# The last pair's gate and rest turned to token rows by VectorE, GpSimd and DMA instead of TensorE

## The chip, the cores and the metric

The kernel runs on one core of a Trainium2 chip. The metric is device time in microseconds (us): the median of the runs of one program. A profile is one more execution, taken by the hardware profiler; its span runs from the first to the last instruction, and the device time of the same execution is a little longer. The engines are TensorE (PE in the profile; its weight loads are PEld), VectorE (DVE), ScalarE (ACT), GpSimd (POOL) and SyncE (SP, which only issues DMAs here). ACT and POOL issue DMAs too. A `q` behind an engine's name in the profile (SPq, ACTq) means its instruction queue.

## The reference

Eight sequences of 512 tokens with 256 features, all float32. Cut to what matters:

```python
nx = layer_norm(x, gamma, beta)
evidence = softmax((nx @ Wq) @ (prototypes @ Wk).T / 16) @ (prototypes @ Wv)
combined = concat([nx, evidence, anchor])             # 768 features
probs = softmax(combined @ router_W + router_b)       # 3 experts
h = silu(combined @ e_w1[e] + e_b1[e])                # 512 hidden features an expert
routed = sum_e probs[e] * (h[e] @ e_w2[e] + e_b2[e])
g = sigmoid(silu(combined @ gate_w1 + gate_b1) @ gate_w2 + gate_b2)
out = x + g * (routed @ out_w + out_b)
```

## The kernel before

The work goes over four pairs of sequences, j = 0 to 3. Within a pair the activations lie with features on the 128 partitions and the 512 tokens along the free dimension, and the big matrix products are made as a 2x2 block scheme over the two sequences of the pair (rows 0 and 1) and the two halves of the features, with seven block products in place of eight; sums and differences of blocks are made by VectorE. `e_w2` and `out_w` are multiplied into one weight beforehand, so that after the hidden layer one more layer of products, in `outputs`, gives `routed @ out_w`.

`outputs(j, steps)` begins with the gate (`hg` tiles, a sigmoid on ACT), and then makes the four results of the pair: `r11` (first half of the features, sequence 0), `r12` (first half, sequence 1), `r21` (second half, sequence 0), `r22` (second half, sequence 1). Each starts as a bias sum on ACT, and TensorE adds block products in PSUM banks `u`, `z`, `y`, twelve products of 128x512 each (`experts`, which calls `product`, L945, twice for each of six steps over the three experts). Two results share bank `u` one after the other: the product for `r22` is added in, VectorE reads it, and then the product for `r21` is added on top of it in the same bank. VectorE adds a bank to its result, multiplies with the gate, turns the result by 32x32 blocks (a stream transpose), and GpSimd adds `x`, which lies in a tile `xb` in the same blocked form (`finish`, L1430 to 1437). `store` (L1425) writes it to the output with four DMAs of 64 KB, in pieces of 128 bytes.

In the first three pairs all four results go this way. The last pair (j = 3) has an order of its own, which the change touches. There `r11`, the first 128 features of sequence 6, is finished with tokens on the partitions, so that it needs no turning at the end: `token_experts` multiplies one 128-token tile of the hidden layer with the weights, twelve products of 128x128 into one PSUM bank, four tiles in all. `finish_rows` then multiplies the bank with the gate (L1511), adds the rest (L1512), both on VectorE, and stores a tile of 128 tokens by one DMA of 64 KB (L1513), tiles 0 and 2 from ACT's queue, tiles 1 and 3 from SP's. "Rest" is what does not wait for this product: `x + gate * (bias sum and the other products of r11)`. The gate and the rest have features on the partitions, and have to be turned to token rows first. Before the change `finish_early` (L1439 to 1445) makes the rest on VectorE (a block transpose of `xb`, a multiplication, an addition), and `turn_rest` (L1494) turns gate and rest on TensorE: eight transposes of 128x128 into two PSUM banks, which ACT copies to the tile `rest` (L1502). `turn_rest` stands between the product for `r22` and the last sum, that for `r21`; the token products follow the last sum. `r21` has been prepared by `finish_early` as well, and `finish_late` (L1452) multiplies the last sum with the gate in place (tile `hg`), adds, turns by blocks, and stores by two DMAs from ACT's queue and two from SP's. The token rows lie in a tile `y_rows` that takes over one of the two buffers `yb`, from which `r12` has been stored.

The order of the work: each engine carries out its instructions in the order in which the code issues them (`manual_schedule`), and the framework puts in the waits between engines, on semaphores. A DMA is issued by an engine's queue when its waits are over, and what stands behind it in that queue waits with it. The DMAs that SP and ACT issue count on eight semaphores, which the framework deals round in the order in which its own plan places the DMAs; a DMA that gets a semaphore whose last owner may not be done yet waits for that owner to land.

Of the kernel before, what the change touches and what calls it, by code (L numbers as in the profile page):

```python
# [8 lines left out]
F32 = mybir.dt.float32  # L9
AF = mybir.ActivationFunctionType  # L10
ALU = mybir.AluOpType
# [5 lines left out]
def kernel(  # L17
# [51 lines left out]
    nc = tc.nc  # L69
    P = 128  # L70
    B, T, H = x.shape
# [3 lines left out]
    NT = T // P  # L75
# [11 lines left out]
    dram = ctx.enter_context(tc.tile_pool(name="dram", bufs=2, space=bass.MemoryType.DRAM))  # L87
# [3 lines left out]
    work = ctx.enter_context(tc.tile_pool(name="work", bufs=2))  # L91
# [8 lines left out]
    def bank(i, name):  # L100
        ps = psum.tile([P, 512], F32, tag=f"b{i}", name=name)
        bank_of[ps.name] = i
        return ps
# [4 lines left out]
    def misc(name):  # L108
        spare.append(spare.pop(0))
        return bank(spare[-1], name)  # L110
# [6 lines left out]
    ident = const.tile([P, P], F32, tag="ident", name="ident")  # L117
# [15 lines left out]
    TB = 32  # L133
# [68 lines left out]
    r = 0  # L202
# [373 lines left out]
    S = {}  # L576
# [366 lines left out]
    def product(ps, lhsT, rhs, start=False):  # L943

        return nc.tensor.matmul(ps, lhsT, rhs, start=start, stop=True, skip_group_check=not start)  # L945
# [46 lines left out]
    def hidden(j, q, k, i):  # L992
        return S["h", i, 2 * q // RC][:, (2 * q + k) % RC, :]
# [344 lines left out]
    def outputs(j, steps):  # L1338
# [7 lines left out]
        hg = [[S["hg", i, k] for i in range(2)] for k in range(2)]  # L1346
# [14 lines left out]
        u, z, y = (bank(i, f"ps_g{n}_{j}") for n, i in (("u", 0), ("z", 2), ("y", 4)))  # L1361
# [23 lines left out]
        def a(q, i, k):  # L1385
            return w2o[:, 2 * q + k, i * P : (i + 1) * P]

        def experts(ps, lhs, k, i, start=False):
            for q in range(NQ):
                product(ps, lhs(q), hidden(j, q, k, i), start=start and q == 0)  # L1390

        def combo(s):
            return lambda q: w2s[:, s, q, :]
# [11 lines left out]
        def bias_sum(role, i, row):  # L1405

            r = work.tile([P, T], F32, tag=role, name=f"{role}_{j}", bufs=1)
            nc.scalar.activation(
                by_side(r), pb[:, row, :, 1, :], AF.Identity, bias=b2o[:, i, 0:1],
                scale=b2o[:, i, 1:2],  # L1410
            )
            for e in range(2, E):
                nc.vector.scalar_tensor_tensor(
                    by_side(r), pb[:, row, :, e, :], b2o[:, i, e : e + 1], by_side(r), ALU.mult, ALU.add
                )
            return r
# [13 lines left out]
        def finish(r, ps, i, row):  # L1430

            yb = work.tile([P, T], F32, tag="yb", name=f"yb_{2 * j + row}_{i}")
            nc.vector.tensor_tensor(r, r, ps, ALU.add)
            nc.vector.tensor_tensor(r, r, S["hg", row, i], ALU.mult)
            nc.vector.transpose(yb, r)  # L1435
            nc.gpsimd.tensor_tensor(yb, yb, S["xb", 2 * j + row][:, i, :], ALU.add)  # L1436
            store(yb, i, row, slice(0, T), (nc.sync,))

        def finish_early(r, i, row):  # L1439

            xb = S["xb", 2 * j + row][:, i, :]
            yb = work.tile([P, T], F32, tag="yb", name=f"yb_{2 * j + row}_{i}")
            nc.vector.transpose(yb, xb)
            nc.vector.tensor_tensor(r, r, S["hg", row, i], ALU.mult)
            nc.vector.tensor_tensor(r, r, yb, ALU.add)
# [6 lines left out]
        def finish_late(r, ps, i, row):  # L1452
# [5 lines left out]
        r11, r22, r12, r21 = (  # L1458
            bias_sum(f"r{i + 1}{row + 1}", i, row) for i, row in ((0, 0), (1, 1), (0, 1), (1, 0))
        )  # L1460
        ug = u
        u, y, z = (bank(i, f"ps_{n}2_{j}") for i, n in ((1, "u"), (3, "y"), (5, "z")))
# [15 lines left out]
        if j + 1 < NP:  # L1478
# [12 lines left out]
            run("P4")  # L1491
            return

        def turn_rest(r):  # L1494

            rest = work.tile([P, 2, NT, P], F32, tag="xg", name="rest", bufs=1)
            for n, part in enumerate((S["hg", 0, 0], r)):
                pt = misc(f"pt_rest_{n}")
                for t in range(NT):
                    ts = slice(t * P, (t + 1) * P)  # L1500
                    nc.tensor.transpose(pt[:, ts], part[:, ts], ident)
                nc.scalar.copy(rest[:, n, :, :].rearrange("p t c -> p (t c)"), pt)  # L1502
            return rest

        def token_experts(ps, t):

            for q in range(NQ):
                product(ps, hidden(j, q, 1, 0)[:, t * P : (t + 1) * P], a(q, 0, 1), start=q == 0)

        def finish_rows(y, rest, ps, t, queue):  # L1510
            nc.vector.tensor_tensor(y, ps, rest[:, 0, t, :], ALU.mult)  # L1511
            nc.vector.tensor_tensor(y, y, rest[:, 1, t, :], ALU.add)  # L1512
            queue.dma_start(out[2 * j, t * P : (t + 1) * P, :P], y)  # L1513

        subtract((0, 1), ((1, 0), (0, 1)))
        experts(z, combo(S4), 1, 1)
        finish_early(r11, 0, 0)
        finish_early(r21, 1, 0)
        finish(r12, z, 0, 1)
        experts(u, lambda q: a(q, 1, 0), 0, 0)  # L1520
        finish(r22, u, 1, 1)
        rest = turn_rest(r11)
        experts(u, lambda q: a(q, 1, 1), 0, 1)
        tokens = [bank(b, f"ps_tokens_{b}")[:, :P] for b in (2, 0, 5, 3)]
        for t in range(NT):
            token_experts(tokens[t], t)
        finish_late(r21, u, 1, 0)
        y = work.tile([P, NT, P], F32, tag="yb", name="y_rows")
        for t in range(NT):
            finish_rows(y[:, t, :], rest, tokens[t], t, nc.sync if t % 2 else nc.scalar)  # L1530


    with tc.manual_schedule(engines=None):
# [85 lines left out]
        for j in range(NP):  # L1619
# [79 lines left out]
            gate_layer(j, within)  # L1699
            half_layers(j)  # L1700
            outputs(j, between)


# [32 lines left out]
```

## Time and profile before

| what | time |
|---|---|
| median of 3 runs | 455.69 us (455.13 to 455.75) |
| the profiled execution, device time | 454.99 us |
| the profiled execution, span | 453.2 us |
| TensorE busy | 448.6 us, 99% of the span |
| VectorE busy | 363.8 us, 80% |
| ACT busy | 214.5 us, 47% |
| GpSimd busy | 96.8 us, 21% |
| mean granted TensorE clock | 1.0 |

The rows of the profile below have the start in us from the beginning of the span, the length in us, the engine, the line of the kernel, the operation, the tiles it writes and reads (out<-in), shapes as partitions x elements, and how many instructions were merged. In brackets stands how long the engine was idle before, and what ended that. The chain of waits is followed back from the last instruction: at each step to what released it, or to the instruction before it on its engine. The waits of SP's queue have the total, the count and the longest.

### The profile page before, as it was taken

To read this page: it belongs to the slowest core of one execution; us is meant where nothing else is said; L and a number is where in the kernel's file an instruction comes from. 1 tells how busy PE (TensorE), PEld (TensorE's weight loads), DVE (VectorE), ACT (ScalarE), POOL (GpSimd) and SP (SyncE) were. 2 spreads that over 40 slices of the span, in tenths; PEclk is the share of its full clock that TensorE was granted. 3 is DMA by queue.
4 is the path that set the end of the run, shared out by engine and by line. 5 is a ranking of instruction groups with operands and counts; after the bars stand their busy time and mean duration, and the time that the engine had idled before them with its cause. 6 is when DMAs were issued, how large, how long until landed. Compare 5 with 4: busy or idle time off the path is not lost.

```text
span 453.2 us, 5537 instructions
## 1 busy us (share of the span) xinstructions
PE 448.6 (99%) x1801; PEld 214.4 (47%) x1801; DVE 363.8 (80%) x698; ACT 214.5 (47%) x378; POOL 96.8 (21%) x157
## 2 busy tenths in 40 slices
PE   9999999999999999999999999999999999999996
PEld 7554444754444444444444544444444444444445
DVE  2878999949698899769789899777979956677983
ACT  3545875463501675466230476658330355557000
POOL 6466600342432200001331310000151310000010
PEclk9999999999999999999999999999999999999999
DMA  8984682354012477203002248301102291000014
GB/s 254 385 177 114 104 251 40 59 124 45 1 29 41 118 176 146 51 0 47 7 10 36 47 154 166 54 0 29 25 0 47 48 210 23 1 0 0 1 17 76
DMA packets 119956, 35.32 MB, mean 78 GB/s; under 512 B 106076, under 2 KB 116376, under 8 KB 119928
## 3 DMA queue, kind: packets, MB, share of 16 engines
q1 hardware_dynamic: 115344, 27.02, 29.0%
q0 software_dynamic: 2656, 7.16, 4.9%
q10 hardware_dynamic: 1928, 0.80, 0.7%
q8 instruction: 14, 0.23, 0.2%
q14 instruction: 14, 0.11, 0.1%
HBM read 27.56 MB, written 7.39 MB: 77 GB/s over the span
## 4 chain that ended last, share of the span: by engine, by line
PE 99%; DVE 0%; issue 0%
PE ps_u L945 45%; PE ps_z L945 20%; PE ps_y L945 14%; PE ps_gu L945 3%; PE ps_vw L824 3%; PE ps_w2o L547 2%; PE ps_s L691 2%; PE ps_gz L945 2%; PE ps_tokens L945 1%; PE ps_late_u L945 1%; PE ps_wake L316 1%; PE ps_v L356 1%; PE ps_m L356 1%; PE ps_gy L945 1%; PE ps_late_z L945 1%; PE pt_x L619 0%
## 5 line engine op out<-in xcount | busy, mean ns | idle before, releaser
L945 PE MATMUL ps_u<-nxT,w 64*128 64x512 f32 (+1 forms) x208 | 96.6, 591 | 0.0
L1024 DVE TENSOR_TENSOR h<-h,pb 128x512 f32<-128x512 f32 x96 | 62.8, 687 | 13.7 <-ACT h L981 13.6
L945 PE MATMUL ps_u<-h,w2o 128*128 128x512 f32 x144 | 63.9, 593 | 0.0
L981 ACT ACTIVATE h<-h,abias 128x512 f32<-128x512 f32 x72 | 49.1, 717 | 27.6 <-DVE h L987 27.6
L945 PE MATMUL ps_y<-nxT,w 64*128 64x512 f32 (+1 forms) x104 | 51.4, 589 | 0.0
L945 PE MATMUL ps_z<-T,ws 64*128 64x512 f32 (+1 forms) x104 | 51.4, 590 | 0.0
L945 PE MATMUL ps_z<-nxT,ws 64*128 64x512 f32 (+1 forms) x104 | 51.3, 589 | 0.0
L945 PEld LDWEIGHTS ps_u<-nxT,w 64*128 64x128 f32 (+1 forms) x208 | 37.2, 187 | 26.4 <-issue 23.1
L945 PE MATMUL ps_u<-T,ws 64*128 64x512 f32 (+1 forms) x104 | 49.4, 589 | 0.0
L945 PE MATMUL ps_u<-T,w 64*128 64x512 f32 x112 | 48.4, 590 | 0.0
L945 PEld LDWEIGHTS ps_u<-h,w2o 128*128 128x128 f32 x144 | 27.3, 190 | 32.8 <-issue 32.3
L945 PE MATMUL ps_z<-h,w2s 128*128 128x512 f32 x96 | 42.5, 592 | 0.0
L945 PE MATMUL ps_z<-wT,vw 64*128 64x512 f32 x78 | 39.1, 589 | 0.0
L990 ACT COPY h<-ps_u 128x512 f32<-128x512 f32 x48 | 27.7, 580 | 22.9 <-PE ps_u L945 22.8
L1436 POOL TENSOR_TENSOR yb<-yb,xb 128x512 f32<-128x512 f32 x14 | 20.6, 1474 | 67.6 <-DVE yb L1435 54.5
L1403 DVE TENSOR_TENSOR h<-h,h 128x1024 f32<-128x1024 f32 x24 | 30.9, 1342 | 0.0
L945 PEld LDWEIGHTS ps_z<-h,w2s 128*128 128x128 f32 x96 | 18.2, 190 | 23.0 <-issue 22.0
L945 PEld LDWEIGHTS ps_y<-nxT,w 64*128 64x128 f32 (+1 forms) x104 | 19.5, 187 | 12.8 <-issue 12.3
L945 PEld LDWEIGHTS ps_z<-nxT,ws 64*128 64x128 f32 (+1 forms) x104 | 19.1, 187 | 12.8 <-issue 9.7
L945 PEld LDWEIGHTS ps_z<-T,ws 64*128 64x128 f32 (+1 forms) x104 | 19.0, 187 | 12.8 <-issue 11.6
L945 PEld LDWEIGHTS ps_u<-T,ws 64*128 64x128 f32 (+1 forms) x104 | 18.4, 187 | 13.2 <-issue 12.3
L945 PEld LDWEIGHTS ps_u<-T,w 64*128 64x128 f32 x112 | 18.3, 187 | 13.2 <-issue 12.5
(271 smaller groups left out, 849.1 us busy)
## 6 DMA issues: line engine op xcount, KB each, us to landing
pb<-pd POOLq DMA_DIRECT2D x8, 768.0 KB, 4.9
xb<-in_x_dram SPq DMA_DIRECT2D x64, 64.0 KB, 2.4
out_dram<-yb SPq DMA_DIRECT2D x56, 64.0 KB, 1.8
x<-in_x_dram SPq DMA_DIRECT2D x24, 128.0 KB, 2.8
xd<-x SPq DMA_DIRECT2D x24, 128.0 KB, 2.3
xg<-xd SPq DMA_DIRECT2D x48, 64.0 KB, 2.5
w<-in_L_xcond_e_w_dram SPq DMA_DIRECT2D x4, 512.0 KB, 7.6
scr_wa<-in_L_xcond_e_w_dram SPq DMA_DIRECT2D x3, 512.0 KB, 10.3
```

Of the source, the lines that this page charges most:

```text
L316: nc.tensor.matmul(ps_wake[0][:, :P], zeros, zeros, start=True, stop=True)
L356: nc.tensor.matmul(ps, w_sb[:, k, m * P : (m + 1) * P], src[:, k, :], start=(k == 0), stop=(k == KH - 1))
L547: nc.tensor.matmul(ps[:, d * H : (d + 1) * H], w2["T"][u % 2][:, c : c + P], ow_sb[:, k, :], start=(k == 0), stop=(k == KH - 1),)
L691: nc.tensor.matmul(ps[side(i, h), g * NH : (g + 1) * NH], mr[:, k, 2 * j + i, g * TB : (g + 1) * TB], S["nxT", 2 * j + i][:, k, h * NH : ( ...
L824: nc.tensor.matmul(ps, vT[:, k, j * 2 * CT : (j + 1) * 2 * CT], w1[:, KH + k, n0:n1], start=(k == 0), stop=(k == KH - 1),)
L945: return nc.tensor.matmul(ps, lhsT, rhs, start=start, stop=True, skip_group_check=not start)
L981: nc.scalar.activation(h, h if src is None else src, AF.Silu, bias=abias[:, c, 2 * j + i : 2 * j + i + 1])
L990: nc.scalar.copy(chunk(n, i, d), part)
L1024: nc.vector.tensor_tensor(h, h, S["pb", j][:, i, :, 2 * q // RC, :], ALU.mult)
L1403: nc.vector.tensor_tensor(d, p, m, ALU.subtract)
L1436: nc.gpsimd.tensor_tensor(yb, yb, S["xb", 2 * j + row][:, i, :], ALU.add)
```

## The change

The gate and the rest of the last pair are no longer turned by TensorE. `turn_rest` multiplies `r11` with the gate (VectorE), turns it by 32x32 blocks into a plane of the tile `nxT`, which is free by then (VectorE), and adds the blocked `x` to it (GpSimd); `turn_gate` turns the gate by blocks into the other plane. `turn_by_rows` writes such a plane with four DMAs of 64 KB to a scratch tensor in device memory, with each token a row, and reads it back with one DMA of 256 KB into the tile `rest`, tokens on the partitions. The four writes of the rest go from SP's and ACT's queue in turn, those of the gate from SP's alone; both reads go from SP's. All this is issued before `r12` is finished, so on SP's queue it stands ahead of the stores of `r12` and `r22`. The eight transposes, their two PSUM banks and ACT's two copies are gone, and so is `finish_early` of `r11`. Token tile 0's twelve products move from behind the last sum to between the last two sums, where the transposes were.

```diff
--- before.py
+++ after.py
@@ -1491,43 +1491,58 @@
             run("P4")
             return
 
+        rest = work.tile([P, 2, NT, P], F32, tag="xg", name="rest", bufs=1)
+
+        def turn_by_rows(n, blocks, queues):
+
+            rd = dram.tile([T, P], F32, tag=f"rest{n}", name=f"rest{n}")
+            by_block = rd.rearrange("(j r) c -> r j c", r=TB)
+            for m in range(P // TB):
+                ms = slice(m * TB, (m + 1) * TB)
+                queues[m % len(queues)].dma_start(
+                    by_block[:, :, ms], blocks[ms, :].rearrange("r (j c) -> r j c", c=TB)
+                )
+            queues[0].dma_start(rest[:, n, :, :], rd.rearrange("(t p) c -> p t c", p=P))
+
+        def turn_gate():
+            blocks = S["nxT", 2 * j][:, 0, :]
+            nc.vector.transpose(blocks, S["hg", 0, 0])
+            turn_by_rows(0, blocks, (nc.sync,))
+
         def turn_rest(r):
-
-            rest = work.tile([P, 2, NT, P], F32, tag="xg", name="rest", bufs=1)
-            for n, part in enumerate((S["hg", 0, 0], r)):
-                pt = misc(f"pt_rest_{n}")
-                for t in range(NT):
-                    ts = slice(t * P, (t + 1) * P)
-                    nc.tensor.transpose(pt[:, ts], part[:, ts], ident)
-                nc.scalar.copy(rest[:, n, :, :].rearrange("p t c -> p (t c)"), pt)
-            return rest
+            blocks = S["nxT", 2 * j][:, 1, :]
+            nc.vector.tensor_tensor(r, r, S["hg", 0, 0], ALU.mult)
+            nc.vector.transpose(blocks, r)
+            nc.gpsimd.tensor_tensor(blocks, blocks, S["xb", 2 * j][:, 0, :], ALU.add)
+            turn_by_rows(1, blocks, (nc.sync, nc.scalar))
 
         def token_experts(ps, t):
 
             for q in range(NQ):
                 product(ps, hidden(j, q, 1, 0)[:, t * P : (t + 1) * P], a(q, 0, 1), start=q == 0)
 
-        def finish_rows(y, rest, ps, t, queue):
+        def finish_rows(y, ps, t, queue):
             nc.vector.tensor_tensor(y, ps, rest[:, 0, t, :], ALU.mult)
             nc.vector.tensor_tensor(y, y, rest[:, 1, t, :], ALU.add)
             queue.dma_start(out[2 * j, t * P : (t + 1) * P, :P], y)
 
         subtract((0, 1), ((1, 0), (0, 1)))
         experts(z, combo(S4), 1, 1)
-        finish_early(r11, 0, 0)
+        turn_rest(r11)
+        turn_gate()
         finish_early(r21, 1, 0)
         finish(r12, z, 0, 1)
         experts(u, lambda q: a(q, 1, 0), 0, 0)
         finish(r22, u, 1, 1)
-        rest = turn_rest(r11)
+        tokens = [bank(b, f"ps_tokens_{b}")[:, :P] for b in (2, 0, 5, 3)]
+        token_experts(tokens[0], 0)
         experts(u, lambda q: a(q, 1, 1), 0, 1)
-        tokens = [bank(b, f"ps_tokens_{b}")[:, :P] for b in (2, 0, 5, 3)]
-        for t in range(NT):
+        for t in range(1, NT):
             token_experts(tokens[t], t)
         finish_late(r21, u, 1, 0)
         y = work.tile([P, NT, P], F32, tag="yb", name="y_rows")
         for t in range(NT):
-            finish_rows(y[:, t, :], rest, tokens[t], t, nc.sync if t % 2 else nc.scalar)
+            finish_rows(y[:, t, :], tokens[t], t, nc.sync if t % 2 else nc.scalar)
 
 
     with tc.manual_schedule(engines=None):
```

## The prediction

> **What bounds the kernel now.** I read the page first, then the chain of waits over the last 28 us, then the timeline of the same stretch, then the waits of SP's own queue, and last the DMA issues.
>
> ```profile
> span 453.2 us, 5537 instructions
> PE 448.6 (99%) x1801; PEld 214.4 (47%) x1801; DVE 363.8 (80%) x698; ACT 214.5 (47%) x378; POOL 96.8 (21%) x157
> PE 99%; DVE 0%; issue 0%
> ```
>
> The page: TensorE is the chain, 99% of it, up to the last microseconds. So whatever leaves TensorE there is gained, as long as the work behind the last product does not grow. The chain of waits from 425 us on (start, length, what):
>
> ```profile
> 432.98 5.15 PE ps_u L945 x12
> 438.13 0.87 PE pt_rest L1501 x8
> 439.01 5.32 PE ps_u L945 x12
> 444.33 5.37 PE ps_tokens L945 x48
> 449.70 0.02 issue
> 449.73 0.30 DVE y_rows L1511
> 450.03 0.02 issue
> 450.05 0.29 DVE y_rows L1512
> ```
>
> The eight transposes are worth 0.87 us of this chain, a group of twelve 128x512 products 5.15, a 128x128 product 5.37 / 48 = 0.112. The timeline of the tail shows who works beside them:
>
> ```profile
> 438.10 1.27 POOL L1436 TENSOR_TENSOR yb<-yb,xb 128x512 f32<-128x512 f32 x1 [8.36 <-DVE yb L1435]
> 438.17 0.69 DVE L1433 TENSOR_TENSOR r<-r,ps_u 128x512 f32<-128x512 f32 x1 [0.30 <-PE ps_u L945]
> 438.89 1.03 DVE L1434 TENSOR_TENSOR r<-r,hg 128x512 f32<-128x512 f32 x1
> 439.40 4.71 SPq L1425 DMA_DIRECT2D out_dram<-yb  x8
> 440.89 1.26 POOL L1436 TENSOR_TENSOR yb<-yb,xb 128x512 f32<-128x512 f32 x1 [1.51 <-DVE yb L1435]
> 446.56 0.93 ACTq L1425 DMA_DIRECT2D out_dram<-hg  x2
> 447.37 0.29 DVE L1512 TENSOR_TENSOR y_rows<-y_rows,rest 128x128 f32<-128x128 f32 x1
> 449.29 1.43 SPq L1513 DMA_DIRECT2D out_dram<-y_rows  x2
> ```
>
> Look at the last two lines. VectorE had token tile 1 ready at 447.66, and SP issued its store at 449.29. SP's waits say why (total us, times, longest):
>
> ```profile
> SPq L1513 <- DMA out_dram<-hg: 1.8, 1, 1.8
> SPq L508 <- DMA xd<-x: 0.8, 2, 0.4
> ```
>
> SP stood 1.8 us until a store that ACT had issued at 446.56 was in memory. There is no data between the two. The framework deals eight DMA semaphores round to all DMAs of SP and ACT, and a DMA may not use its semaphore before the DMA that had it last has landed. Here this cost nothing, because the last store waited for VectorE anyway. It is the line on which my forecast rests. The DMA issues (KB each, median us to landing):
>
> ```profile
> out_dram<-hg ACTq DMA_DIRECT2D x2, 64.0 KB, 3.4
> out_dram<-y_rows SPq DMA_DIRECT2D x2, 64.0 KB, 1.6
> ```
>
> **The change part by part.** The sum is made against the profiled execution: span 453.2, device time 454.99, which is 0.70 under the median of 455.69. I add the difference to the median.
>
> TensorE. The eight transposes go: -0.87. Token tile 0 moves ahead of the last sum: 12 x 0.112 = 1.34, nothing in total. So the last sum ends 1.34 - 0.87 = 0.47 later (444.33 to 444.80), and the last token product 0.87 earlier (449.70 to 448.83). The transposes also covered a wait: the last sum adds into the bank that VectorE (L1433) reads until 438.86. Now token tile 0 covers it until 438.13 + 1.34 = 439.47, 0.6 us to spare. GpSimd's new addition can stretch VectorE by about what the 1.03 us row shows over 0.69, 0.34, part of which falls into VectorE's 0.30 idle before L1433. So this wait costs nothing; without that cover it would cost the excess over 0.6.
>
> VectorE loses a transpose, a multiplication and an addition of r11 (0.70 + 0.65 + 0.69) and gains a multiplication and two transposes (0.65 + 0.70 + 0.70): 0. ACT loses two copies that nobody on the chain waited for: 0. GpSimd gains one addition of 1.27 in time in which it was idle (8.36 us before 438.10).
>
> A rule of the Trainium skill speaks against the move: "VectorE: DVE Perf Modes", Rules for kernel authors, has a 128x128 transpose go to TensorE where PSUM will do, and The three transpose paths gives 390 ns for one (bf16). By that figure eight are an estimated 3.1 us, and the gain on TensorE would be 3.1; the chain says 0.87, and I keep the row.
>
> SP's queue. Ahead of its twelve old issues of the tail come two stores of the rest, a load, four stores of the gate, a load; ACT gets the other two stores of the rest. VectorE frees the rest at 431.88 + 0.63 + 0.70 = 433.2, GpSimd has it at about 434.7. Its four stores are issued by 435.6 and land by about 438 (434.7 plus 1.7 to 3.4, the ends of the 64 KB stores here). SP waits for them with everything behind it, then issues the load, then the gate's four stores (four took 444.11 - 442.15 = 1.96, so 0.49 each) by 440.5; they land at about 442.3, and SP stands again. Load at 442.4; nearest rows for 256 KB in 512-byte pieces are 64 KB at 1.6 and the 256 KB of the context at 4.2, so it is there between 444.0 and 446.6. Then the four stores of r12, to 445.0 instead of 441.4, landed by about 447. The first token product on VectorE needs all of this, and can start at 444.80 + 2.13 = 446.9 in any case. So the two round trips are covered, by a hair for the store of r12, whose buffer the token rows take over. If one came late it would shift VectorE's four pairs (0.6 each).
>
> The semaphore. I counted the eight semaphores through the built program of the changed kernel, in the order in which the waits on them stand. ACT's first store of the last sum's result (hg) takes the fifth, and its next owner is the second of the four stores of r22, on SP. In the queue of SP that store stands ahead of two more of r22, two of hg and the two token stores. So SP, which gets there at 445.5, must stand until a store has landed that can only be issued at 446.56 + 0.47 = 447.03. Behind it are six more issues, the last of them the last store of the kernel:
>
> - ACT's hg store issued: 447.03
> - landed: 1.7 (the fastest 64 KB store here) to 2.7 (449.29 - 446.56 for this very store, then beside two of SP's). SP is silent now, so I take the middle, 2.2: 449.23, and 0.05 until SP goes on
> - six issues further at 0.48 (0.40 to 0.55): 2.9, the last token store at 452.2; it has been ready since about 449.5
> - landing 1.6 as SP's token stores had it (to 1.9, the median of the stores of L1425): 453.8
> - from the last landing to the end 1.2, as before (450.37 + 1.58 to 453.2): 455.0.
>
> That is +1.8 on the span. All low ends: 453.98, +0.8. All high ends: 456.2, +3.0. The 0.87 that TensorE gives back is lost before it reaches the end, as the last store no longer waits for TensorE.
>
> Another rule meets this: "DMA: Bandwidth & Descriptors", Rules for kernel authors, wants a semaphore dedicated to a DMA. The kernel has the opposite, and the 1.8 us of SP's wait agree with the rule. With dedicated ones the sum would be the -0.9 of the first rival below.
>
> **The rivals.**
>
> - The gain reaches the end. If the hold is not there on the chip, SP is done with r22 at 447.0, with hg at 448.0 and with token tile 1 at 448.5, and the last store is ready at 448.83 + 0.65 = 449.5, 0.87 earlier: 454.8. For it: TensorE is the chain in 99%. Against: it needs ACT's hg store in memory before SP comes to the second store of r22 at 445.5, and its data is made at 447.0. Only another dealing of semaphores than in the program I counted does that.
> - The hold is short. Landing in 1.7 and issues of 0.40, as for the low ends: +0.8, 456.5, and less if the last issues follow faster still: within 0.9 of before. For it: first issues after a wait take 0.33 to 0.35. Against: a run of four took 0.49 each.
> - The rows come late. If a round trip takes so long that the first token product starts after 452.2 - 4 x 0.6 = 449.8, 2.9 us later than reckoned, VectorE instead of SP sets the last store, and each microsecond above counts in full: 459 and more. For it: two dependent trips, and a startup load of 256 KB that took 17 us to land. Against: the kernel's own store-and-load of x loses SP 0.4 us at most per trip, and the DMA engines are idle from 432 to 439.
>
> **How the numbers follow.** Forecast, held on the semaphore: 0.80. Gain reaches the end: 0.07. Short hold that ends within 0.2%: 0.08. Late rows: 0.05. The predicted time is 455.69 + 1.8 = 457.5. The forecast's own range by its ends is 456.5 to 458.7; taking in the short hold below and leaving out the case in which all high ends meet, the range is 456.3 to 458.4. About 0.2% (0.9 us) is what a measurement of this kernel can tell from no change: slower 0.80 + 0.05, within 0.08, faster 0.07.
>
> **What would show it.** In the changed kernel's profile the chain must lose pt_rest and have twelve ps_tokens between two groups of ps_u; ps_tokens must end near 448.8. SP's waits must show L1425 held by hg, some 3.7 us, with the second store of yb for r22 near 449.2, and the last y_rows store near 452, 2 us or more after its VectorE operation ended. VectorE's first y_rows product must start near 447 with no long wait for a DMA. I am wrong if SP's run of eight yb stores is issued before 447.5, if ps_u waits for VectorE after token tile 0, or if y_rows on VectorE starts after 449.8.

## The result and the profile after

| | before | after |
|---|---|---|
| median, same chip (6 runs each) | 455.35 us (454.9 to 455.75) | 456.71 us (456.48 to 457.26) |
| ratio after / before, 95% interval | | 1.0035 [1.0024, 1.0045] |
| profiled execution, span | 453.2 us | 454.5 us |
| profiled execution, device time | 454.99 us | 456.48 us |

The change costs 1.36 us by the medians; 1.8 was forecast. A second measurement of the same kernel (run e11 below) gave 1.0049 [1.0035, 1.0063], that is 2.25 us by its medians. So the forecast lies between the two, and slower by more than 0.2% holds in both. From the common point that is introduced below, the two profiled executions lose nearly the same, 1.4 and 1.5 us.

The page of the changed kernel, its span, its busy times and the engines' shares of the chain:

```profile
span 454.5 us, 5534 instructions
PE 447.2 (98%) x1793; PEld 212.9 (47%) x1793; DVE 364.2 (80%) x698; ACT 213.4 (47%) x376; POOL 98.4 (22%) x158
PE 95%; DMA 2%; SPq 1%; DVE 1%; issue 0%; DVEq 0%
```

TensorE has 8 instructions and 1.4 us less, and the span is 1.3 us longer: TensorE no longer is the chain to the end. DMA and SP's queue have come into it. The chain of waits from 425 us on (start, length, what) shows where:

```profile
432.86 5.16 PE ps_u L945 x12
...
438.05 0.70 DVE r L1433
...
440.19 2.22 DMA rest<-nxT
...
442.49 0.38 SPq L1505
...
444.65 2.37 DMA out_dram<-yb
...
447.31 0.30 DVE y_rows L1525
...
449.21 0.29 DVE y_rows L1526
```

It leaves TensorE at 438.02, behind the sum for `r22`, and runs over VectorE, the gate's four stores and the stores of `r12` to the token rows. One step of it is an inference of the view and no dependence: from VectorE's L1433 to the gate's stores (L1502). The timeline below has their first issue start at 438.50, while L1433 ran until 438.74, and they read nothing of what L1433 makes. SP came to them behind the load of the rest, which it had issued at 438.03. The chain ends at 449.50 with VectorE's last instruction, 0.84 earlier than in before (450.05 + 0.29 = 450.34). But the span is longer, so the end is not set by what this view follows: it follows engines' work, and what lies behind 449.50 is DMA issues. The timeline of the tail has them:

```profile
433.33 1.26 POOL L1516 TENSOR_TENSOR nxT<-nxT,xb 128x512 f32<-128x512 f32 x1 [3.72 <-DVE nxT L1515]
437.85 1.50 PE L945 MATMUL ps_tokens<-w2o,h 128*128 128x128 f32 x12
438.03 0.38 SPq L1505 DMA_DIRECT2D rest<-rest  x1
438.05 0.69 DVE L1433 TENSOR_TENSOR r<-r,ps_u 128x512 f32<-128x512 f32 x1
438.50 2.19 SPq L1502 DMA_DIRECT2D rest<-nxT  x4
439.18 5.32 PE L945 MATMUL ps_u<-h,w2o 128*128 128x512 f32 x12
442.91 7.06 SPq L1425 DMA_DIRECT2D out_dram<-yb  x8
446.73 0.87 ACTq L1425 DMA_DIRECT2D out_dram<-hg  x2
447.31 0.29 DVE L1525 TENSOR_TENSOR y_rows<-ps_tokens,rest 128x128 f32<-128x128 f32 x1 [0.61 <-DMA out_dram<-yb]
449.21 0.29 DVE L1526 TENSOR_TENSOR y_rows<-y_rows,rest 128x128 f32<-128x128 f32 x1
450.06 1.03 SPq L1425 DMA_DIRECT2D out_dram<-hg  x2
451.20 0.93 SPq L1527 DMA_DIRECT2D out_dram<-y_rows  x2
```

SP's eight stores of `r12` and `r22` took 4.71 us before, from 439.40; now they take 7.06 from 442.91, and ACT's stores of `hg` fall into that time. The last token store is issued at 451.74, 2.2 us after VectorE had the rows ready. SP's waits from 430 us on (total, times, longest):

```profile
SPq L1505 <- DMA rest<-nxT: 4.1, 3, 2.4
SPq L1425 <- DMA out_dram<-hg: 2.8, 1, 2.8
```

The second line is the wait that the forecast named: a store of `yb` stands 2.8 us until a store of `hg`, with which it shares no data, has landed.

### The profile page after: what moved, and what is told of

It is laid out like the page before. It is cut to its first block, busy times and chain, and to the rows that moved or that the text cites. A ratio compares the mean times of both kernels' runs of the same rounds, so it can differ in the third digit from the quotient of the medians.

```text
span 454.5 us, 5534 instructions
## 1 busy us (share of the span) xinstructions
PE 447.2 (98%) x1793; PEld 212.9 (47%) x1793; DVE 364.2 (80%) x698; ACT 213.4 (47%) x376; POOL 98.4 (22%) x158
## 4 chain that ended last, share of the span: by engine, by line
PE 95%; DMA 2%; SPq 1%; DVE 1%; issue 0%; DVEq 0%
PE ps_u L945 43%; PE ps_z L945 20%; PE ps_y L945 14%; PE ps_gu L945 3%; PE ps_vw L824 3%; PE ps_w2o L547 2%; PE ps_s L691 2%; PE ps_gz L945 2%; PE ps_late_u L945 1%; DMA scr_ctx<-in_ctx_dram 1%; PE ps_v L356 1%; PE ps_m L356 1%; PE ps_gy L945 1%; PE ps_late_z L945 1%; DMA out_dram<-yb 1%; DMA rest<-nxT 0%
```

## The experiments

One thing has to be known before single executions are compared. The first 19 us or so, in which the weights arrive, differ from execution to execution; from there on the kernels that share their instructions keep step to about 0.01 us until the tail. The start of the twelve `ps_u` products ahead of the turning (432.98 in the chain of before, 432.86 in that of after) shows by how much a whole execution is shifted. TensorE's granted clock is no part of it: it is 1.00 in every stretch from 0 to 450 us, in before and in after. Below, "tail" is the span less that shift, compared with before's: for after 454.5 - 453.2 + 0.13 = +1.4.

| run | ratio to before, 95% interval | span | shift | tail |
|---|---|---|---|---|
| after | 1.0035 [1.0024, 1.0045] | 454.5 | -0.13 | +1.4 |
| e11, after again | 1.0049 [1.0035, 1.0063] | 455.4 | +0.66 | +1.5 |
| e1, `hg` from GpSimd and SP | 1.0035 [1.0022, 1.0047] | 455.1 | +0.15 | +1.7 |
| e2, token rows in a buffer of their own | 1.0064 [1.0051, 1.0077] | 456.4 | +0.40 | +2.8 |
| e3, `hg` from ACT alone | 1.0058 [1.0045, 1.0072] | 455.9 | -0.09 | +2.8 |
| e4, token tile 0 put back | 1.0040 [1.0027, 1.0053] | 455.2 | +0.15 | +1.9 |
| e5, `hg` from SP alone | 1.0021 [1.0012, 1.0030] | 454.4 | +0.44 | +0.8 |
| e6, round trips earlier | 1.0028 [1.0017, 1.0040] | 455.0 | +0.88 | +0.9 |
| e7, e6 and gate's trip on ACT | 1.0002 [0.9993, 1.0011] | 453.7 | +0.74 | -0.2 |
| e8, before, token tile 0 moved alone | 1.0015 [1.0006, 1.0023] | 454.0 | +0.32 | +0.5 |
| e9, e7, `hg` from ACT, tokens from SP | 0.9984 [0.9975, 0.9993] | 452.7 | +0.07 | -0.6 |
| e10, before with e9's queues | 1.0007 [0.9998, 1.0015] | 453.3 | +0.10 | 0.0 |

Each ratio is against runs of before on the same chip. The differences of the medians agree with the tails within 0.5 us, except for e11 (2.25 us against 1.5), whose profiled execution also has a start-up 0.66 us longer than before's.

Three theories stood against each other. In the expectations H is the hold: SP stands until a store of ACT has landed, because the two share a semaphore. Q is the queue: the round trips that SP now makes ahead of its old stores, and the number of issues behind them, set the end by themselves. D is VectorE: the token rows come late, because their buffer waits for the stores of `r12`. Besides, TensorE's own end was on trial (e4).

**e1: the hold's owner taken off the shared semaphores.** GpSimd's DMAs do not count on the semaphores that SP and ACT share: in e1's trace they have 116 and 117, those of SP and ACT 108, 110 and 120 to 125.

```diff
-            store(g, i, row, slice(0, T), (nc.scalar, nc.sync))
+            store(g, i, row, slice(0, T), (nc.gpsimd, nc.sync))
```

> The changed kernel, but the two stores of hg that ACT issued are issued by GpSimd, whose DMAs do not count on the eight semaphores of SP and ACT. SP's queue keeps every issue and both round trips. Theory H (SP is held by a semaphore that ACT's hg store owned): the hold is gone, SP runs through, the last token store waits for VectorE again and is issued near 449.5: span about 452.4, 0.8 less than before and 2.1 less than the changed kernel. Rival Q (eight more issues and two round trips on SP make the last store late): unchanged, 1.3 over before. Rival D (the token rows come late on VectorE, held 0.61 us by the stores of r12): unchanged as well.

The time did not move. The timeline of SP's queue in e1 says that two things happened at once:

```profile
443.11 4.40 SPq L1425 DMA_DIRECT2D out_dram<-yb  x8
447.61 1.00 SPq L1425 DMA_DIRECT2D out_dram<-hg  x2
448.71 1.73 SPq L1527 DMA_DIRECT2D out_dram<-y_rows  x2
```

The eight stores now run through in 4.40 us instead of 7.06, and the last token store is issued at 449.82, 0.36 after its rows were ready (449.46), where after had 2.2. So the hold is gone, and with it nearly all of SP's delay: the same trips and the same issues behind them do not make SP 2.2 us late, which speaks against Q. But the end did not follow. GpSimd's closing wait for its own DMAs ran from 447.76 to 454.27, beyond the last landing of SP's and ACT's stores (452.62), and set the end. Its stores went in 4 KB packets (median 0.58 us), and beside them the last token store took 2.8 us to land. The expectation left the price of GpSimd's DMAs out.

**e2: token rows not in a buffer of `yb`.** This takes away VectorE's real wait for the stores of `r12`.

```diff
-        y = work.tile([P, NT, P], F32, tag="yb", name="y_rows")
+        y = work.tile([P, 3, NT, P], F32, tag="T", name="y_rows", bufs=1)[:, 0]
```

> The changed kernel, but y_rows has a buffer of its own and need not wait until r12 is stored; a true wait of VectorE is taken away and nothing is added. The semaphores are dealt otherwise by that: the last owner before the fourth store of r12 is now ACT's first hg store. H: SP is held at the same moment, near 448.5, but with nine issues behind the held one instead of seven: 0.9 slower than the changed kernel, about 2.2 over before, span 455.4, although VectorE finishes its rows 0.6 earlier. Q: as the changed kernel. D: 0.6 faster than the changed kernel.

VectorE started its rows without a wait for a store and had the last ready at 449.70, yet no kernel here is slower (e3 has the same tail, +2.8). So D falls. SP's waits in e2:

```profile
SPq L1425 <- DMA out_dram<-hg: 4.1, 1, 4.1
```

The edit changed the framework's plan, and so the dealing of the semaphores: now the last store of `r12` is the held one (to 449.40), eight issues stand behind it instead of six, and the last store is issued 4.25 us after the release (3.19 in after). A true wait was removed, the hold moved two places forward, and the hold set the time, as H has it. H's own figure was 0.9 over after, and measured were 1.4 by the tails: the eight issues took 1.06 us more than after's six, and the release came 0.3 later, because ACT's first `hg` store took 2.11 us to land instead of 1.81.

**e3: two issues fewer on SP.** Q expects a gain from it.

```diff
-            store(g, i, row, slice(0, T), (nc.scalar, nc.sync))
+            store(g, i, row, slice(0, T), (nc.scalar,))
```

> The changed kernel, but all four stores of hg are issued by ACT, so SP has two issues fewer. The fourth store of r12 now gets the semaphore of ACT's first hg store, and VectorE's token rows wait for that store, whose buffer they take over. H: SP is held until 448.5 at that store, VectorE starts its rows only near 450.3, and the last store is issued near 452.4: span about 455.3, 0.8 over the changed kernel. Q: two issues of 0.5 fewer, 1.0 under the changed kernel. D: as the changed kernel.

It is 1.4 us slower than after by the tails. The reason stands in the two lines of e3's waits and its timeline:

```profile
SPq L1425 <- DMA out_dram<-hg: 3.8, 1, 3.8
```

```profile
450.97 0.29 DVE L1525 TENSOR_TENSOR y_rows<-ps_tokens,rest 128x128 f32<-128x128 f32 x1 [4.24 <-DMA out_dram<-yb]
452.14 1.41 SPq L1527 DMA_DIRECT2D out_dram<-y_rows  x2
```

Here the held store is again one of `r12`, whose buffer the token rows take over, so VectorE stands 4.24 us as well, and starts its rows 0.7 us later than H had reckoned (450.3). Fewer issues on SP, and a later end: second evidence against Q.

**e4: token tile 0 back behind the last sum.** If TensorE's order sets the end, this kernel loses about a microsecond; if the hold sets it, it gains, since `hg` is made earlier.

```diff
-        token_experts(tokens[0], 0)
         experts(u, lambda q: a(q, 1, 1), 0, 1)
-        for t in range(1, NT):
+        for t in range(NT):
             token_experts(tokens[t], t)
```

> The changed kernel, but token tile 0 stays behind the last sum as before, so nothing covers the reading of bank u by VectorE. The dealing of semaphores at the held store is the same. H: TensorE waits 0.7 for VectorE between the two sums, yet the last sum starts 0.4 earlier than in the changed kernel and hg with it, so everything behind the hold comes 0.4 earlier: span about 454.1, although TensorE's last product ends 1.0 later. If TensorE set the end: 1.0 slower than the changed kernel. Q: no difference.

The timeline shows TensorE's side as the forecast's sentence on the bank has it:

```profile
439.06 5.42 PE L945 MATMUL ps_u<-h,w2o 128*128 128x512 f32 x12 [0.78 <-DVE r L1433]
```

Without the cover TensorE stood 0.78 us for VectorE, and its last product ended a microsecond later; `hg` was out 0.3 earlier than in after, counted from the common point. Neither shows in the time: 1.0040 cannot be told from after's 1.0035 and 1.0049. VectorE had its last row ready at 450.49, and SP issued the last store at 452.52, so TensorE does not set the end. The gain of 0.4 that was expected is not there, and the tail is 0.5 longer; the third store of `r22` was held too, by ACT's second `hg` store, which the expectation had overlooked, and its issue took 1.2 us. Why it took so long is open; an instruction fetch of 8 KB lay 1.2 us on a DMA engine at that moment, which fits but was not tried.

**e5: all `hg` stores from SP.** No store of ACT is left that SP could stand for ahead of the token rows; two issues more on SP.

```diff
-            store(g, i, row, slice(0, T), (nc.scalar, nc.sync))
+            store(g, i, row, slice(0, T), (nc.sync,))
```

> The changed kernel, but all four stores of hg are issued by SP, so SP has two issues more and ACT owns no semaphore that a store of r12, r22 or hg gets next. What is left is a hold of token tile 1's store by ACT's store of token tile 0, near 450.1. H: SP runs from r12 through hg without a hold, the last store follows at about 450.6: span about 453.4, 1.1 under the changed kernel, 0.2 over before. Q (the length of SP's queue): two more issues, 1.0 over the changed kernel. The GpSimd path of the first experiment is not used, so its long drain at the end must be gone: with it the end would not come before 454.5.

SP's queue in e5 and its remaining wait:

```profile
443.43 4.41 SPq L1425 DMA_DIRECT2D out_dram<-yb  x8
447.94 2.13 SPq L1425 DMA_DIRECT2D out_dram<-hg  x4
451.24 0.83 SPq L1527 DMA_DIRECT2D out_dram<-y_rows  x2
```

```profile
SPq L1527 <- DMA out_dram<-y_rows: 1.1, 1, 1.1
```

The eight stores of `yb` again run through, in 4.41. With two issues more than after the tail is 0.6 shorter. That is against Q a third time. H's number was missed by 0.6: the hold that the expectation had named, of token tile 1's store by ACT's store of tile 0, ended at 451.19 instead of 450.1 (450.5 with this execution's shift), as ACT's store took 2.78 us to land.

**e6: both round trips earlier.** They move ahead of the sums that prepare `r12`, so they end before the stores of `r12` are due.

```diff
-        turn_rest(r11)
-        turn_gate()
         finish_early(r21, 1, 0)
...
+        turn_rest(r11)
+        turn_gate()
         subtract((0, 1), ((1, 0), (0, 1)))
```

> The changed kernel, with the turning of rest and gate issued ahead of the subtraction that needs 3.5 us of VectorE, so both round trips start about 3.5 us earlier; the same issues on the same queues. The dealing of semaphores moves: now SP's first hg store must wait for ACT's second hg store, with three issues behind it instead of six. H: held until about 449.1, last store near 450.5, span about 453.2: 1.3 under the changed kernel and 0.0 to before. Q (round trips too late): the trips end before r12 is ready and nothing else delays SP, so the last store waits for VectorE: span 452.2, 1.0 under before.

The eight stores of `yb` start at 441.05 instead of 442.91, in spite of a start-up that was a microsecond later than after's. SP's waits in e6, and its queue beside ACT's stores:

```profile
SPq L1425 <- DMA out_dram<-hg: 5.0, 1, 5.0
```

```profile
441.05 4.58 SPq L1425 DMA_DIRECT2D out_dram<-yb  x8
447.81 0.87 ACTq L1425 DMA_DIRECT2D out_dram<-hg  x2
450.68 0.93 SPq L1425 DMA_DIRECT2D out_dram<-hg  x2
```

SP is done earlier and only stands longer, now with its own first `hg` store, until ACT's second `hg` store has landed. The tail is 0.5 shorter than after's, with three issues behind the held one instead of six. H had expected no loss against before and Q a gain of 1.0, so both missed: +0.9. The trips end long before they are needed, and a hold still sets the end, so the trips' time is not what costs. H's miss is in the length of the hold: ACT's two `hg` stores took 2.50 and 2.44 us to land, although SP issued nothing from 445.6 to 450.68.

**e7: e6, and the gate's trip from ACT's queue.** Besides taking five DMAs off SP, this moves the dealing.

```diff
-            turn_by_rows(0, blocks, (nc.sync,))
+            turn_by_rows(0, blocks, (nc.scalar,))
```

> As the sixth experiment, and the gate's round trip goes through ACT's queue, which is idle then. Token tile 1's store on SP waits for ACT's first hg store, token tile 3's for nothing that is late. H: the hold ends near 449.2 with one issue behind it, the last store is issued near 449.7: span about 452.5, 0.7 under before, 2.0 under the changed kernel. Q: 452.2. If the round trips cost anything beside other work, it would show as a wait of VectorE's token rows for a DMA; none is expected.

```profile
SPq L1527 <- DMA out_dram<-hg: 2.0, 1, 2.0
```

The hold is still there (SP's waits above), but it now falls on token tile 1's store with one issue behind it, as in before. The time is that of before. H had expected 0.7 less; the hold ended at 450.50 instead of 449.2 (449.9 with this execution's shift), since ACT's first `hg` store took 2.83 us to land.

**e8: before, with only token tile 0 moved.**

```diff
-        experts(u, lambda q: a(q, 1, 1), 0, 1)
         tokens = [bank(b, f"ps_tokens_{b}")[:, :P] for b in (2, 0, 5, 3)]
-        for t in range(NT):
+        token_experts(tokens[0], 0)
+        experts(u, lambda q: a(q, 1, 1), 0, 1)
+        for t in range(1, NT):
```

> The kernel before with one part of the change alone: token tile 0's products stand between the last two sums, behind the transposes, which stay on TensorE. The last sum ends 1.3 later, the last token product as before. All theories: 0.0 to before (within 0.2), since the last store waits for the last token product; hg comes 1.3 later, and the semaphore that its first store from ACT holds goes to the last token store, which is ready only after it has landed (about 450.0 against 450.3).

It was expected to be free, and costs 0.15% [0.06, 0.23]. In the profiled execution the last token store, held until 450.72 by ACT's first `hg` store, is issued only 0.1 later than before on the common scale, but lands in 1.99 us instead of 1.58. `hg` comes out 1.2 us later here and its stores overlap the token rows'. That the overlap is the cause is argued from this one execution, not shown.

**e9: the hold made short.** e7, with all `hg` stores from ACT and all token stores from SP.

```diff
-            store(g, i, row, slice(0, T), (nc.scalar, nc.sync))
+            store(g, i, row, slice(0, T), (nc.scalar,))
...
-            finish_rows(y[:, t, :], tokens[t], t, nc.sync if t % 2 else nc.scalar)
+            finish_rows(y[:, t, :], tokens[t], t, nc.sync)
```

> As the seventh experiment (trips earlier, the gate's on ACT's queue), and all hg stores are issued by ACT, all token stores by SP. Only token tile 2's store then gets a semaphore that ACT's first hg store had, and that one lands near 449.0, when the tile is just ready; the last token store waits for nothing but VectorE. H: the last store is issued near 449.5, span about 452.3 in an execution that starts like the one before: 0.9 under before, ratio 0.998, 2.2 under the changed kernel. If the round trips through memory or GpSimd's addition cost something that is still hidden behind the holds: 0.2 under before or more.

This one is faster than both kernels: 454.52 us against 455.17 for before. Its chain of waits is TensorE's again to the end, with the eight transposes gone:

```profile
433.05 5.15 PE ps_u L945 x12
438.20 1.34 PE ps_tokens L945 x12
439.54 5.23 PE ps_u L945 x12
444.77 4.03 PE ps_tokens L945 x36
448.80 0.02 issue
448.82 0.30 DVE y_rows L1525
```

Its waits of SP, from 438 us on:

```profile
SPq L1425 <- POOL yb L1436: 5.4, 2, 4.8
SPq L1527 <- DVE y_rows L1525: 2.8, 1, 2.8
SPq L1527 <- DMA out_dram<-hg: 0.9, 1, 0.9
```

SP mostly waits for data. A hold is left, 0.9 us on tile 2's store, and it puts the last token store at 449.93, where its rows were ready at 449.44. Those 0.5 us cover the 0.3 that the tail of -0.6 lacks to the -0.9 expected.

**e10: before, with e9's queues.** The same two lines as in e9's diff, applied to before.

> The kernel before, transposes on TensorE, with the queues of the ninth experiment alone (all hg stores from ACT, all token stores from SP). The last store waits for VectorE as before: 0.0 to before, within 0.2. If the ninth is faster only because of its queues, this one is as fast as that.

1.0007 [0.9998, 1.0015], tail 0.0. So e9's gain does not come from the queues of these stores alone. Against e10, e9 has 455.45 - 454.52 = 0.93 us less by the medians and 0.6 by the tails, and the eight transposes were 0.87 on before's chain.

**e11: the changed kernel a second time,** beside e9 and e10.

> The changed kernel again, on the chip of the ninth and tenth experiments: 1.4 over before, as measured. Counted from the twelve products that precede the turning, the last token store must again be issued about 19.2 us later and ACT's first hg store land about 1.8 us after its issue.

The tail repeats to 0.1: `hg` is issued at 447.52, the held store of `r22` at 449.35, the last token store at 452.67. That is 19.0 us behind the common point (433.65), where after had 18.9 and the forecast 19.2 (452.2 - 432.98). ACT's first `hg` store landed 1.81 us after its issue, as in after.

Over the series H named the held store and its owner in advance, but for a second hold in e4. Where the hold moved to an earlier store (e2, e3) SP's last store came later than in after, and where it was gone or short (e1, e5, e7, e9) it came earlier, counted from the common point. So the hold is shown as the cause. Its cost was not reckoned well: H's figures were too low in e2 to e7 and in e9, by 0.3 (e9) to 1.0 us (e4), in part because the landing that ends a hold took between 1.8 and 2.8 us.

## Why the prediction was right, and where its sizes were off

Direction, mechanism and range held. Step by step, with the profiled execution of after (0.13 us ahead of the forecast's scale, so 0.13 is to be added to its times before they are compared):

- *TensorE gains 0.87, the last sum ends 0.47 later.* The token products ended at 448.52 (forecast 448.83). `hg` came out 0.30 later than in before, not 0.47, counted from the common point. The forecast had the move of token tile 0 at nothing in total; e8 has 0.15% for it alone, in before's order. In after it could not be seen, as the hold set the end.
- *Token tile 0 covers the wait for bank u.* TensorE waits for nothing from 425 us on, and in e4, without the cover, 0.78. Right. The multiplication beside GpSimd's new addition (L1444) took 0.84 us, where the forecast's sum had 0.65; that is within the 0.34 it allowed.
- *The round trips are covered by a hair.* The rest ready 434.6 (434.7), the gate's stores landed 442.41 (442.3), its load landed 445.45 (444.0 to 446.6), `r12` stored 447.02 (447). VectorE then waited 0.61 us and started at 447.31 (446.9). The hair lay on the other side, at no cost, because SP was later still. Without the hold it could have cost up to about 0.4 us by an estimate: the last token product was done at 448.52, two VectorE operations of 0.3 us each would have had its row at 449.1, and it was ready at 449.50. No run shows this alone.
- *The hold.* It is where it was put, on the second store of `r22`, held by ACT's first `hg` store, with six issues behind it. Term by term:

| term | forecast | after |
|---|---|---|
| ACT's `hg` store issued | 447.03 | 446.73 |
| its landing | 2.2 (1.7 to 2.7) | 1.81 |
| SP goes on | 449.28 | 448.55 |
| six issues, to the last token store | 2.9 | 3.19 |
| last token store issued | 452.2 | 451.74 |
| its landing | 1.6 | 1.58 |
| to the end | 1.2 | 1.15 |
| span | 455.0 | 454.5 |

The mis-sized term is the landing of the `hg` store: taken as the middle of 1.7 and 2.7, it was near the lower end, 0.4 us less. The six issues were missed the other way, by 0.3 us, so that part of the closeness of 455.0 to 454.5 is luck. The forecast chose the middle although it saw that "SP is silent now". That this silence made the store fast is not shown. With SP issuing nothing, ACT's first `hg` store landed in 1.80 to 1.81 us in after, e3, e4 and e11, but in 2.11 in e2 and 2.50 in e6. With SP issuing at the same time it took 1.87 (e10), 2.44 (e9), 2.67 (before and e8) and 2.83 (e7). What decides within these ranges stays open. SP's hold was 2.8 us instead of the 3.7 of the forecast, since SP came later to it and was released earlier.

- *The gain reaches the end* (the first rival, -0.87 and 454.8). It fell for this kernel on exactly the condition that it named. e9 shows that it was about right on the size: with only a short hold most of the transposes' 0.87 does arrive, 0.93 us against e10 by the medians and 0.6 by the tails, in a kernel that takes 454.52 us.
- *The hold is short.* The rival's 1.7 for the landing came nearly true (1.81), but not its 0.40 for an issue: six took 0.53 each.
- *The rows come late.* No: 447.31, far from 449.8. In e3 it happened, at 450.97, because the hold fell on a store of `r12`.

The Trainium skill's page "DMA: Bandwidth & Descriptors" asks under Rules for kernel authors for a semaphore dedicated to a DMA. These runs show how long SP stood where the framework shares them: 2.8 us (after), 3.8 (e3), 4.1 (e2), 5.0 (e6), for DMAs without data between them. What a hold costs depends on what stands behind it: 1.8 us cost nothing in before. A kernel with dedicated semaphores was not run; e9 only chose queues so that the dealing did little harm.

## What to carry to other kernels

When work is taken off the engine that bounds a kernel and given to DMAs, look at the queue that issues the last stores: which semaphore each of them gets, who had it last, when that owner's data exists, and how many issues stand behind. Where the framework deals semaphores over several queues, count that before costing anything else; here kernels with the same arithmetic lay between 1.0064 and 0.9984, and the slowest (e2, e3 and the changed kernel itself in e11) had a hold of 2.7 us or more with several issues behind it. When a hold is reckoned, take the whole range of the landing that ends it, and not one run's value. And a change that loses can hold a gain: the same change with its trips issued earlier, the gate's trip on ACT's queue, the `hg` stores all on ACT's and the token stores all on SP's is the fastest version here.

## What the runs showed of the hardware and the framework beyond that

- The landing of one 64 KB store in 128-byte pieces (ACT's first `hg` store) varied between 1.80 and 2.83 us over the kernels of this series. It was 1.80 to 2.50 with SP's queue silent and 1.87 to 2.83 with SP issuing at the same time, so one measured landing is a poor guide to the next kernel's.
- An edit far from the semaphores moves them. A buffer of its own for the token rows (e2) cost 1.4 us of tail against after, though it removed a wait.
- Stores from GpSimd as a way round (e1) bring a closing wait of 6.5 us of their own.
- Start-up alone shifted whole executions by -0.13 to +0.88 us, several times what separates some of these kernels. Only from the common point on can single executions be compared.
